# Weaving the two expert layers of neighbouring steps in a graph-and-experts kernel, with gate scores of two tiles in one bank and masks ten chunks ahead

## The chip, the cores and the metric

The kernel runs on one core of one Trainium2 chip. The time is device microseconds of one execution of the whole program, the median over several executions. Next to it stands one profiled execution, from which every row, wait and window below is read.

## What is computed

A graph layer is followed by a layer of eight experts, of which each node uses two. There are 6250 nodes with 256 features and 106,250 edges, sorted by their target node.

```python
deg = jnp.maximum(segment_sum(ones, dst, 6250), 1.0)
norm = deg ** -0.5
h = layernorm(x) @ W.T + b                      # 256 -> 256
x = x + norm * segment_sum((norm * h)[src], dst, 6250)
y = layernorm(x)
top, idx = top_k(y @ Wg.T + bg, 2)              # 8 experts, 2 for each node
p = softmax(top)
for e in range(8):                              # 256 -> 1024 -> 256
    x = x + combine(p, idx, e) * (relu(y @ W1[e].T + b1[e]) @ W2[e].T + b2[e])
```

## The kernel before

The prologue counts the degrees, scales the nodes and writes them to HBM as a table (`table`). Then the main loop runs over the edges in 831 chunks of 128, one chunk to a slot `s` of the program. The order of all work is written out by hand: what follows is put into the engines' queues in the order in which this loop calls it, and each engine takes its own queue in order.

**A slot.** It issues the gather of chunk `s + 6` on GpSimd (`gather`, L403: 128 rows of the table into one of 24 `rows` buffers), builds the mask of chunk `s + MASKS` on VectorE (`mask`, L410, MASKS is 6) and adds chunk `s` up on TensorE (`add_up`, L417: mask times rows into the bank `ps`). A row buffer comes free when its chunk has been added up, so gathers can lead TensorE by at most 24 chunks. A mask buffer comes free eight chunks after its use (`bufs=MASKS + 8`).

**Tasks of a tile.** A tile is 128 nodes, and 17 chunks on average hold the edges of one. From the slot at which its sums are complete, tasks follow at fixed distances (`STAGES`, L659): the sum is turned (L505), goes through the linear layer (`linear`, L517), gets its scores, chooses two experts (VectorE), is ranked (L585, L586), sorted by expert (`sort`, L649) and sent to queues in HBM, one for each expert (`send`, L672, eight stores on SyncE). The graph layer's part of the scores comes from `linear`; the part of the input `x` is worked out for two tiles at a time, early in the loop, by `inputs_turned` (L449, L452) and two slots later `inputs_scored` (L456 to L462). The latter takes one tile `ph` for each of the two node tiles, four matmuls into it, and one ScalarE copy of 128x8 out of it (L462).

**Steps.** A step is 256 queued rows of one expert (128 rows in the first nine and the last six steps of the 60). `choose` picks the expert, `load_first` (L723), `load_rows` (L732) and `load_second` (L737) load the first weights `w1` (1028 KB), the rows `xT` and the second weights `w2` (1152 KB). `up` (L757 to L767) is one of eight pieces of the first layer: four matmul instructions into one of the two `ph` banks, and a ReLU on ScalarE that empties it into `hid`. `down` (L769 to L780) is one of eight pieces (four for 128 rows) of the second layer, four matmul instructions into `py`; `leave` adds the bias on VectorE and stores to `yq`. `w1`, `w2` have three buffers each, `hid` two, `xT` four.

**The planner.** `next_piece` (L879) runs all `up` pieces of step `done` and then all its `down` pieces; `cur` counts them. The main loop (L894 to L912) gives each slot a credit of SLOT - CHUNK = 1025 (nanoseconds, less the planned cost `busy` of the slot's tasks), keeps at most SPARE = 2000 of it, and issues pieces while credit is positive and the step is `ready`: its `w2` has been issued and slot `earliest[step]` is reached. A piece is charged 915 (`up`) or 870 (`down`) for 256 rows. In steady state steps are due 17 slots apart.

**The tail.** After the last chunk (L913 on) one piece is issued in each turn, and between them the results are read back from `yq` by indirect gathers on GpSimd (`read_back`, L857), weighed and added (L865), and stored. `DONE` says after which step which tiles may be read. Loads are kept three steps ahead of `done` and `gone` (L934 to L943).

Of the kernel before, what the change touches and what calls it, by code (L numbers as in the profile page):

```python
# [7 lines left out]
F32 = mybir.dt.float32  # L8
# [6 lines left out]
AF = mybir.ActivationFunctionType  # L15
# [4 lines left out]
P = 128  # L20
# [8 lines left out]
NE = 8  # L29
H = 1024  # L30
HB = H // P
# [14 lines left out]
ROWS_OF = [n for s, n in STREAM] + list(TAIL)  # L46
USUAL = len(ROWS_OF)
# [7 lines left out]
PIECES = {FT: (915, 870), P: (600, 870)}  # L55
# [5 lines left out]
SPREAD = 4.0  # L61
AHEAD = 6
UP = 2.0 ** 11
MASKS = 6
ROWS = 24
HC = 64
GROUP = 7
# [6 lines left out]
LATER = 1 << 17  # L74
TURNED, PLACED, SORTED, SENT = 5, 17, 22, 24
LEAD = (13, 12)


COPIES = 3
# [70 lines left out]
def in_order(ctx: ExitStack, tc: tile.TileContext, g: Shared):  # L150

    nc = tc.nc
# [190 lines left out]
    psp = ctx.enter_context(tc.tile_pool(name="fpsp", bufs=2, space=PSUM))  # L343
# [6 lines left out]
    wg = keep.tile([P, 2, NE], F32, name="wg")  # L350
# [8 lines left out]
    xg = keep.tile([P, NT, NE], F32, name="xg")  # L359
# [7 lines left out]
    t0 = 0  # L367
    for step, t1 in DONE:
        nc.vector.memset(bounds[:, t0:t1, :], float(START[step + 1]))
        t0 = t1  # L370
# [83 lines left out]

    def inputs_scored(t0, t1):
        xT = turned_inputs.pop(t0)  # L456
        for t in range(t0, t1):
            px = psp.tile([P, NE], F32, name="ph")
            for k in range(2):
                nc.tensor.matmul(px, xT[:, k, (t - t0) * P:(t - t0 + 1) * P], wg[:, k, :],  # L460
                                 start=(k == 0), stop=(k == 1))
            nc.scalar.activation(xg[:, t, :], px, AF.Copy)  # L462

    kept = {w: (WINDOWS[w - 1][0] % P, WINDOWS[w][0] - WINDOWS[w - 1][0]) for w in range(1, len(WINDOWS))}
    keeps = {}
# [209 lines left out]
    steps = {}  # L675
# [63 lines left out]
    def fetch(step):  # L739

        for _ in choose(step):
            yield
            if step in steps and "w1" not in steps[step] and step < done + (cur >= HB) + 3:
                load_first(step)
        while "w1" not in steps[step]:
            if step < done + (cur >= HB) + 3:
                load_first(step)
            else:
                yield
        while sent < steps[step]["known"]:  # L750
            yield
        load_rows(step)
        while step >= gone + 3:
            yield
        load_second(step)

    def up(step, b):  # L757
        f = steps[step]
        w1 = f["w1"]
        n = ROWS_OF[step]  # L760
        if b == 0:
            f["hid"] = work.tile([P, HB, FT], F32, name="hid")
        ph = psp.tile([P, FT], F32, name="ph")
        for k in range(2):
            nc.tensor.matmul(ph[:, :n], w1[:, k * H + b * P:k * H + (b + 1) * P], f["xT"][:, :n, k],  # L765
                             start=(k == 0), stop=(k == 1))
        nc.scalar.activation(f["hid"][:, b, :n], ph[:, :n], AF.Relu, bias=w1[:, 2 * H + b:2 * H + b + 1])  # L767

    def down(step, i, s):  # L769
        f = steps[step]  # L770
        a = i // 4
        if i % 4 == 0:
            f["py"] = psp.tile([P, D], F32, name="py")
        for b in (2 * (i % 4), 2 * (i % 4) + 1):
            nc.tensor.matmul(f["py"], f["hid"][:, b, a * P:(a + 1) * P], f["w2"][:, b * D:(b + 1) * D],  # L775
                             start=(b == 0), stop=(b == HB - 1))
        if i % 4 == 3:
            plan_at(s + 1, leave, step, a, f["py"], f["w2"])
        if i == 4 * ROWS_OF[step] // P - 1:
            del steps[step]  # L780
# [32 lines left out]
    earliest, busy = {}, {}  # L813
# [17 lines left out]
    s = 1  # L831
# [12 lines left out]
    chosen = loaded1 = loaded2 = len(STREAM)  # L844
    all_sent = FROM[NT - 1] + SENT + 1

    cur = 0
    done = gone = 0

    def results(t0, t1, bound):  # L850

# [21 lines left out]
        if t1 == NT:  # L873
            engine.dma_start(g.out[(NT - 1) * P:N, :], g.xr[:LAST, NT - 1, :])

    def ready(s):
        return done < USUAL and "w2" in steps.get(done, {}) and s >= earliest.get(done, 0)

    def next_piece(s):  # L879

        nonlocal cur, done
        step = done
        if not ready(s):
            return
        if cur < HB:
            up(step, cur)
        else:
            down(step, cur - HB, s)
        cur += 1
        if cur == HB + 4 * ROWS_OF[step] // P:  # L890
            done += 1
            cur = 0

    with tc.manual_schedule():  # L894
        with rowp as rowpool:
            for c in range(AHEAD):
                gather(c)
            for c in range(MASKS):
                mask(c)
            credit = 0  # L900
            for s in range(NC):
                if s + AHEAD < NC:
                    gather(s + AHEAD)
                if s + MASKS < NC:
                    mask(s + MASKS)
                add_up(s)
                for fn, args in tasks.pop(s, []):
                    fn(*args)
                credit = min(credit + SLOT - CHUNK - busy.get(s, 0), SPARE)
                while credit > 0 and ready(s):  # L910
                    credit -= PIECES[ROWS_OF[done]][cur >= HB]
                    next_piece(s)  # L912
        with tc.tile_pool(name="ftail", bufs=2) as pool:  # L913
            s = NC
            pend = []
            plan = list(DONE)
            got = asked = allowed = stored = 0
            latest = 0
            since = {}

            def take():
                nonlocal got, stored
                t, j, yb = pend.pop(0)[1]
                add_in(t, j, yb)
                got += 1
                if got == 2 * stored + 11:
                    store(stored, stored + 4, nc.gpsimd)
                    stored += 4

            while done < USUAL or tasks or len(plan) > 1 or asked < 2 * allowed or pend:  # L930
                for fn, args in tasks.pop(s, []):
                    fn(*args)
                if s > all_sent and s > max(STREAM)[0] + 6:
                    if chosen < min(USUAL, done + 4):  # L934
                        run(choose(chosen))
                        chosen += 1
                    if loaded2 < min(loaded1, gone + 3):
                        load_second(loaded2)
                        loaded2 += 1
                    if loaded1 < min(chosen, done + (cur >= HB) + 3):  # L940
                        load_first(loaded1)
                        load_rows(loaded1)
                        loaded1 += 1  # L943
                was = done
                next_piece(s)
                if done > was:
                    since[was] = s
                if len(plan) > 1 and done > plan[0][0] and s >= since.get(plan[0][0], 0) + 6 \
                        and asked == 2 * allowed:
                    step, t1 = plan.pop(0)  # L950
                    results(allowed, t1, float(START[step + 1]))
                    allowed = t1
                    latest = step
                if asked < 2 * allowed and s % (4 if s > all_sent else 2):
                    pend.append((s, read_back(pool, rowat, asked // 2, asked % 2, latest)))
                    asked += 1

                if pend and (done == USUAL or len(pend) > 10 or s >= pend[0][0] + 8):
                    take()
                s += 1  # L960

            results(allowed, NT, float(START[USUAL]))
            late = work.tile([P, NT, 2], F32, name="late", bufs=1)
            missed = work.tile([P, 2], F32, name="missed")
            nc.vector.tensor_tensor(late, at, bounds, op=OP.is_ge)
            nc.vector.tensor_reduce(missed[:, 0:1], late, op=OP.add, axis=mybir.AxisListType.XY)
            nc.vector.tensor_reduce(missed[:, 1:2], most, op=OP.max, axis=mybir.AxisListType.X)
            nc.vector.tensor_scalar(missed[:, 1:2], missed[:, 1:2], float(SLOTS), None, op0=OP.is_gt)  # L970
            nc.vector.tensor_add(missed[:, 0:1], missed[:, 0:1], missed[:, 1:2])
            nc.vector.tensor_add(missed[:, 0:1], missed[:, 0:1], g.outside)
            ones = work.tile([P, 1], F32, name="ones")
# [547 lines left out]
```

## Time and profile before

| | |
|---|---|
| median of 3 runs | 1326.41 us (1326.34 to 1326.47) |
| the profiled execution | 1612.34 us, of which 1610.5 us is the span of the profile |
| mean granted TensorE clock in it | 0.879 |
| TensorE matmuls busy | 1241.0 us, 77% of the span |
| VectorE, ScalarE busy | 980.9 us (61%), 397.7 us (25%) |
| GpSimd busy | 901.2 us (56%) |
| gathers of the main loop | 831, 0.949 us each |

The profiled execution is 21.6% longer than the median run. Rows are read as: line, engine, operation, tiles written and read, shapes, count, busy time, mean length in ns, idle time of the engine just before, and what ended most of that idle time. A wait whose cause the profile doesn't show is put down to "issue" or "remote". `ph` is the tile of both `up` and `inputs_scored`.

### The profile page before, as it was taken

The page shows a single profiled execution, that of the slowest core. Times are in us where ns is not written, and L with a number is a line of the kernel's source. Part 1 is how long each engine was busy: PE and PEld are TensorE (multiplying, and loading weights), DVE is VectorE, ACT ScalarE, POOL GpSimd, SP SyncE. Part 2 cuts the span into 40 slices and gives each one's busy share as a digit, 9 for nine tenths or more (in the row PEclk, how much of TensorE's full clock was granted, in tenths as well). Part 3 has the DMA queues.
Part 4 walks back from the last instruction along what each step waited for, and adds up shares of the span by engine and source line. Part 5 has one row for each costly group of instructions (what it writes and reads, how often), then busy time and mean ns, then how long its engine had stood idle before and what let it go on. Part 6 is the DMA issues. An engine that isn't in the chain of part 4 may idle for free.

```text
span 1610.5 us, 24215 instructions
## 1 busy us (share of the span) xinstructions
PE 1241.0 (77%) x6304; PEld 937.4 (58%) x6304; DVE 980.9 (61%) x5416; ACT 397.7 (25%) x963; POOL 901.2 (56%) x983
## 2 busy tenths in 40 slices
PE   5237768874778898888888787889888888778894
PEld 5215546663556565655656565656656666567683
DVE  8711556665657676767667666666666665574542
ACT  1602222221221222222222222222222222121231
POOL 1075665656656566666666566656666664236533
PEclk9965767997979899999899898989899998988997
DMA  7432358785667666667767666757677676559784
GB/s 248 161 105 82 102 141 282 258 288 143 204 190 225 190 210 207 218 205 216 214 202 224 200 213 215 225 186 219 209 220 217 202 220 211 176 201 365 252 302 142
DMA packets 159197, 333.81 MB, mean 207 GB/s; under 512 B 26804, under 2 KB 105864, under 8 KB 143688
## 3 DMA queue, kind: packets, MB, share of 16 engines
q1 hardware_dynamic: 111372, 201.66, 37.0%
q0 software_dynamic: 46864, 129.82, 28.0%
q8 instruction: 52, 0.85, 0.2%
q14 instruction: 97, 0.79, 0.2%
q10 hardware_dynamic: 812, 0.68, 0.1%
HBM read 277.55 MB, written 54.50 MB: 206 GB/s over the span
## 4 chain that ended last, share of the span: by engine, by line
PE 56%; issue 11%; DVE 11%; another core or an unknown queue 11%; DMA 5%; ACT 3%; SPq 2%; POOL 1%; ACTq 0%; POOLq 0%; DVEq 0%
PE ph L765 23%; PE py L775 13%; PE ps L417 10%; PE pt L517 3%; PE ph L460 2%; DMA yb<-fyq,rowat 2%; DMA xT<-fhq 2%; ACT hid L767 1%; SPq L672 1%; PE px L649 1%; PE px L449 1%; PE pt L505 1%; PE count L216 1%; DVE mask L410 1%
## 5 line engine op out<-in xcount | busy, mean ns | idle before, releaser
L403 POOL DMA_INDIRECT rows<-ftable,src x831 | 789.0, 949 | 487.2 <-PE ps L417 190.0
L765 PE MATMUL ph<-xT,w 128*128 128x256 f32 (+1 forms) x1920 | 510.1, 405 | 189.4 <-issue 82.3
L765 PEld LDWEIGHTS ph<-xT,w 128*128 128x128 f32 x1920 | 366.4, 212 | 320.5 <-issue 146.4
L775 PE MATMUL py<-w,hid 128*128 128x256 f32 x1680 | 415.7, 381 | 0.0
L767 ACT ACTIVATE hid<-ph,w 128x256 f32<-128x256 f32 (+1 forms) x480 | 210.8, 446 | 633.8 <-PE ph L765 206.2
L775 PEld LDWEIGHTS py<-w,hid 128*128 128x128 f32 x1680 | 319.7, 191 | 70.3 <-issue 1.9
L417 PE MATMUL ps<-rows,mask 128*128 128x512 f16 x831 | 322.0, 416 | 42.8 <-DMA rows<-ftable,src 31.5
L410 DVE TENSOR_SCALAR mask<-col_b,rel 128x128 f16<-128x128 bf16 x831 | 200.8, 265 | 32.2 <-remote 11.7
L857 POOL DMA_INDIRECT yb<-fyq,rowat x98 | 94.6, 965 | 122.4 <-DMA w<-in_W 36.7
L417 PEld LDWEIGHTS <-mask 128*128 128x128 f16 x831 | 88.2, 109 | 76.9 <-issue 34.6
L524 DVE SCALAR_TENSOR_TENSOR xr<-pt,norm,xr 128x256 f32<-128x256 f32 x49 | 23.7, 483 | 151.4 <-PE pt L517 67.0
L787 DVE TENSOR_TENSOR y<-py,w 128x256 f32<-128x256 f32 x105 | 44.1, 420 | 101.5 <-PE py L775 35.4
L484 DVE SCALAR_TENSOR_TENSOR rolled<-rolled,keep,ps 128x256 f32<-128x256 f32 x149 | 70.7, 475 | 42.9 <-PE ps L417 23.3
L499 ACT ACTIVATE whole<-rolled 32x256 f32<-32x256 f32 (+2 forms) x156 | 63.9, 410 | 124.9 <-DVE rolled L487 61.6
L460 PE MATMUL ph<-wg,turned 128*128 128x8 f32 x196 | 40.8, 336 | 50.2 <-ACT turned L452 31.9
L460 PEld LDWEIGHTS ph<-wg,turned 128*128 128x128 f32 x196 | 39.6, 297 | 64.4 <-ACT turned L452 39.6
L487 DVE TENSOR_TENSOR rolled<-ps,rolled 128x256 f32<-128x256 f32 x150 | 63.7, 424 | 15.7 <-DVE rolled L484 6.8
L865 DVE SCALAR_TENSOR_TENSOR xr<-yb,prob,xr 128x256 f32<-128x256 f32 x98 | 45.7, 482 | 41.3 <-DMA yb<-fyq,rowat 40.1
L588 ACT ACTIVATE h2s<-h 128x256 f16<-128x256 f32 x49 | 20.3, 415 | 186.1 <-DVE h L579 104.5
L517 PE MATMUL pt<-gw,uT 128*128 128x264 f32 x196 | 61.9, 445 | 5.4 <-ACT uT L510 3.4
L517 PEld LDWEIGHTS pt<-gw,uT 128*128 128x128 f32 x196 | 44.4, 228 | 21.2 <-issue 5.5
L216 PE MATMUL count<-oh,ol 128*16 128x8 bf16 (+2 forms) x898 | 29.0, 174 | 21.8 <-DVE oh L205 18.0
(187 smaller groups left out, 1128.2 us busy)
## 6 DMA issues: line engine op xcount, KB each, us to landing
w<-in_W SPq DMA_DIRECT2D x60, 1152.0 KB
w<-in_W SPq DMA_DIRECT2D x60, 1028.0 KB
fhq<-ordered SPq DMA_DIRECT2D x392, 64.0 KB
fyq<-y SPq DMA_DIRECT2D x105, 128.0 KB
rows<-ftable,src POOLq DMA_INDIRECT x831
xT<-fhq SPq DMA_DIRECT2D x45, 256.0 KB
out<-xr POOLq DMA_DIRECT2D x11, 512.0 KB
xr<-in_x SPq DMA_DIRECT2D x6, 896.0 KB
```

The costliest lines, as they stand in the source:

```text
L403: nc.gpsimd.indirect_dma_start(out=rows[c], out_offset=None, in_=table[:, :], in_offset=bass.IndirectOffsetOnAxis(ap=g.src[:, c:c + 1], ax ...
L410: nc.vector.tensor_scalar(masks[c], g.col_b[:, r:r + P], g.rel[:, c:c + 1], None, op0=OP.is_equal)
L417: nc.tensor.matmul(sums[w], masks.pop(c), rows.pop(c), start=(c == chunks[0]), stop=(c == chunks[-1]))
L460: nc.tensor.matmul(px, xT[:, k, (t - t0) * P:(t - t0 + 1) * P], wg[:, k, :], start=(k == 0), stop=(k == 1))
L484: nc.vector.scalar_tensor_tensor(new, rolled, keeps[kept[w]], ps[:, 0:D], op0=OP.mult, op1=OP.add)
L487: nc.vector.tensor_add(new, ps[:, D:2 * D], new)
L499: nc.scalar.activation(whole[t][p0:p1, :], new[p0:p1, :], AF.Copy)
L517: nc.tensor.matmul(pl, uT[:, k, :], gw[:, k, :], start=(k == 0), stop=(k == 1))
L765: nc.tensor.matmul(ph[:, :n], w1[:, k * H + b * P:k * H + (b + 1) * P], f["xT"][:, :n, k], start=(k == 0), stop=(k == 1))
L767: nc.scalar.activation(f["hid"][:, b, :n], ph[:, :n], AF.Relu, bias=w1[:, 2 * H + b:2 * H + b + 1])
L775: nc.tensor.matmul(f["py"], f["hid"][:, b, a * P:(a + 1) * P], f["w2"][:, b * D:(b + 1) * D], start=(b == 0), stop=(b == HB - 1))
L857: r = nc.gpsimd.indirect_dma_start(out=yb, out_offset=None, in_=yq[0:START[upto + 1], :], in_offset=bass.IndirectOffsetOnAxis(ap=where[:, ...
```

## The change

A step's first layer is issued in turn with the second layer of the step before it. `next_kind` decides: if both an `up` piece of step `upped` and a `down` piece of step `done` may run, they alternate, with `up` first; an `up` may start only when the step before last is through its second layer (`upped <= done + 1`) and its rows have been issued. A `down` that hasn't begun waits when the next step's `up` is due within HOLD = 10 slots. `inputs_scored` puts the scores of two tiles into one `ph` tile and empties it with one ScalarE copy. MASKS goes from 6 to 10, and the mask buffers from 14 to 18. The conditions for loads are counted in `upped` in place of `done + (cur >= HB)`.

```diff
-MASKS = 6
+MASKS = 10
+HOLD = 10
...
     def inputs_scored(t0, t1):
         xT = turned_inputs.pop(t0)
+        px = psp.tile([P, 2, NE], F32, name="ph")
         for t in range(t0, t1):
-            px = psp.tile([P, NE], F32, name="ph")
             for k in range(2):
-                nc.tensor.matmul(px, xT[:, k, (t - t0) * P:(t - t0 + 1) * P], wg[:, k, :],
+                nc.tensor.matmul(px[:, t - t0], xT[:, k, (t - t0) * P:(t - t0 + 1) * P], wg[:, k, :],
                                  start=(k == 0), stop=(k == 1))
-            nc.scalar.activation(xg[:, t, :], px, AF.Copy)
+        nc.scalar.activation(xg[:, t0:t1, :], px[:, :t1 - t0], AF.Copy)
...
-            if step in steps and "w1" not in steps[step] and step < done + (cur >= HB) + 3:
+            if step in steps and "w1" not in steps[step] and step < upped + 3:
                 load_first(step)
...
-    def ready(s):
-        return done < USUAL and "w2" in steps.get(done, {}) and s >= earliest.get(done, 0)
+    def next_kind(s):
+
+        first = upped < USUAL and upped <= done + 1 and "xT" in steps.get(upped, {}) and s >= earliest.get(upped, 0)
+        second = done < upped and "w2" in steps.get(done, {})
+        if first and second:
+            return "down" if was == "up" else "up"
+        if first:
+            return "up"
+        soon = 0 < earliest.get(upped, 0) - s <= HOLD and upped <= done + 1 and curd == 0
+        return "down" if second and not soon else None

     def next_piece(s):

-        nonlocal cur, done
-        step = done
-        if not ready(s):
-            return
-        if cur < HB:
-            up(step, cur)
-        else:
-            down(step, cur - HB, s)
-        cur += 1
-        if cur == HB + 4 * ROWS_OF[step] // P:
-            done += 1
-            cur = 0
+        nonlocal curu, curd, done, upped, was
+        was = next_kind(s)
+        if was == "up":
+            up(upped, curu)
+            curu += 1
+            if curu == HB:
+                upped, curu = upped + 1, 0
+        if was == "down":
+            down(done, curd, s)
+            curd += 1
+            if curd == 4 * ROWS_OF[done] // P:
+                done, curd = done + 1, 0
+        return was
...
-                while credit > 0 and ready(s):
-                    credit -= PIECES[ROWS_OF[done]][cur >= HB]
-                    next_piece(s)
+                while credit > 0:
+                    of = upped, done
+                    kind = next_piece(s)
+                    if not kind:
+                        break
+                    credit -= PIECES[ROWS_OF[of[kind == "down"]]][kind == "down"]
...
-                    if chosen < min(USUAL, done + 4):
+                    if chosen < min(USUAL, upped + 4):
...
-                    if loaded1 < min(chosen, done + (cur >= HB) + 3):
+                    if loaded1 < min(chosen, upped + 3):
```

More of the change, by code (lines that the diff above doesn't have):

```diff
@@ L742, in fetch @@
             yield
-            if step in steps and "w1" not in steps[step] and step < done + (cur >= HB) + 3:
+            if step in steps and "w1" not in steps[step] and step < upped + 3:
                 load_first(step)
         while "w1" not in steps[step]:
-            if step < done + (cur >= HB) + 3:
+            if step < upped + 3:
                 load_first(step)
@@ L845, in in_order @@
     all_sent = FROM[NT - 1] + SENT + 1
-    cur = 0
-    done = gone = 0
+    curu = curd = 0
+    done = gone = upped = 0
+    was = None
     def results(t0, t1, bound):
@@ L874, in store @@
             engine.dma_start(g.out[(NT - 1) * P:N, :], g.xr[:LAST, NT - 1, :])
-    def ready(s):
-        return done < USUAL and "w2" in steps.get(done, {}) and s >= earliest.get(done, 0)
-    def next_piece(s):
-        nonlocal cur, done
-        step = done
-        if not ready(s):
-            return
-        if cur < HB:
-            up(step, cur)
-        else:
-            down(step, cur - HB, s)
-        cur += 1
-        if cur == HB + 4 * ROWS_OF[step] // P:
-            done += 1
-            cur = 0
+    def next_kind(s):
[7 more added lines that the diff above has]
+        return "down" if second and not soon else None
+    def next_piece(s):
+        nonlocal curu, curd, done, upped, was
[11 more added lines that the diff above has]
+        return was
     with tc.manual_schedule():
@@ L943, in in_order @@
                         loaded1 += 1
-                was = done
+                over = done
                 next_piece(s)
-                if done > was:
-                    since[was] = s
+                if done > over:
+                    since[over] = s
                 if len(plan) > 1 and done > plan[0][0] and s >= since.get(plan[0][0], 0) + 6 \
```

## The prediction

> **What bounds the kernel now.** I read the page first, then busy time by windows, then who waited for whom on TensorE and GpSimd, then the timeline of single slots and the chain of waits.
>
> The windows show a main loop in which one engine is nearly full:
>
> ```profile
> 1000.00:1100.00 100.00, 86.82 (x363) 64.03 (x364) 65.85 (x367) 25.62 (x62) 59.78 (x64) 0.90 0.67 204
> 1100.00:1200.00 100.00, 84.68 (x363) 62.51 (x362) 64.74 (x391) 24.21 (x58) 62.16 (x66) 0.91 0.69 213
> 1200.00:1300.00 100.00, 85.94 (x377) 63.41 (x376) 63.44 (x377) 22.64 (x54) 63.15 (x67) 0.93 0.70 219
> ```
>
> Columns are TensorE matmuls, weight loads, VectorE, ScalarE, GpSimd (busy us, instructions), granted clock, DMA share, GB/s. TensorE is busy 85 to 87%, and the fifth column counts the gathers: 64 to 67 in 100 us, 1.53 us a chunk, 26 us for the 17 chunks of a step.
>
> GpSimd isn't the bound of this execution; it waits for row buffers that TensorE hasn't emptied:
>
> ```profile
> L403 POOL DMA_INDIRECT rows<-ftable,src x831: 940/946/1191, 81.6 to 1357.9; - x167
>   PE ps L417: 190.0, 165
>   issue: 170.7, 536
>   remote: 64.6, 42
> ```
>
> But its own pace, when nothing holds it, is close behind:
>
> ```profile
> 98.21 0.95 POOL L403 DMA_INDIRECT rows<-ftable,src  x1 [0.30 <-issue]
> 99.46 0.95 POOL L403 DMA_INDIRECT rows<-ftable,src  x1 [0.30 <-issue]
> ```
>
> 1.25 us from start to start. The chain of waits gives TensorE's cost of undisturbed pieces:
>
> ```profile
> 819.98 0.90 PE ph L765 x4
> ...
> 822.89 0.22 PE ps L417
> 823.11 0.89 PE pt L517 x4
> ...
> 824.22 0.86 PE py L775 x4
> ```
>
> A first-layer piece takes 0.90 us, a second-layer piece 0.86, a chunk 0.22, `linear` 0.89. So 17 chunks with a step cost 17 x 0.22 + 8 x 0.90 + 8 x 0.86 = 17.8, plus `linear` 0.89, sort 0.45 and turning 0.22 from the same chain, and half of an input pair (1.57 planned for scoring and 0.43 for turning, so 1.0): 20.4 us, 1.20 us a chunk. TensorE undisturbed would be just quicker than the gathers (21.25 us for 17). It takes 26, because it stops:
>
> ```profile
> PE ph L765 <- issue: 74.8, 53, 5.9
> PE ph L765 <- ACT hid L767: 59.4, 25, 6.1
> PE ph L765 <- DMA xT<-fhq: 13.2, 9, 4.5
> PE ps L417 <- DVE rolled L487: 7.8, 2, 6.2
> ```
>
> These are TensorE's waits from 200 to 1350 us (us, times, longest). In that window it is idle 215 us (1150 less 934.5 busy, summed from the windows), and 134 us of it lie before first-layer pieces that wait for a ReLU, or for something unseen. Second-layer pieces wait for nothing. The timeline shows it: from 824.05 on, eight `down` pieces with their chunks run without a gap, while the `up` pieces of the same step, from 805.87, have holes of 3.8 and 0.7 us.
>
> **What the Trainium skill says.** "TensorE: Matmul & The Clock Gate", Part 1 on the HAM clock gate: after an idle window of about 3.4 us the array falls to half clock, and a busy window brings it back. The trace agrees: after the 3.8 us hole at 807.8 the matmuls start 0.43 us apart instead of 0.225, until about 819. So a hole is paid for again. The same page, on engine queue depths: ScalarE and VectorE are strict first-in first-out. Here too: the sort's eviction, the copies `whole`, `uT` and `h2s` (0.4 to 0.6 us each) stand in ScalarE's queue between the ReLUs, and `h2s` alone sat 94 us waiting for VectorE's `h`. "PSUM — Partial Sum Buffer", the four PSUM rules: a group's first matmul clears the written bits of its whole bank. Two score groups in one bank are safe as they run one after the other; no time follows from it.
>
> **Profiled time and median.** The sum below stands against the execution of 1612.34 us (span 1610.5 and 1.8 around it). The median is 286 us less, so most of these waits can't exist there, and a saving in the profile mustn't be carried over whole. I work out what is left. The first gather starts at 81.6. At 1.25 us, 831 gathers take 1039, so the loop ends at 1120, the last chunk 4 later. In the tail stand seven `down` pieces (6.0), seven steps of 256 rows at 14.1 (98.6), six of 128 rows at
>
> ```profile
> 1540.19 4.66 PE L765 MATMUL ph<-xT,w 128*128 128x128 f32 x32
> 1544.69 3.61 PE L775 MATMUL py<-w,hid 128*128 128x256 f32 x16
> ```
>
> about 8.3 (49.6), some 5 for the last tiles, and 22 from the last `down` piece (1589) to the end: 181. Together 1305, 1307 with the 1.8. Only 19 us of the median's 1326 are then losses that TensorE's order can reach. If the 0.30 us between gathers, or part of it, is due to profiling, TensorE itself is the limit: 656 chunks with full steps save 0.05 each (33), and the 175 before them about 17, the floor is 1257 and 69 us can be reached. I take the middle, 44.
>
> **The change part by part.**
>
> *Weaving.* It adds and removes no instruction. Between two `up` pieces now lies a `down` piece (0.86) and often a chunk (0.22), so a ReLU (0.47) may come up to 1.08 us later before its bank is missed. The 78 waits of the two first rows average 1.7 us; at most 78 x 1.08 = 84 us go, 39% of the 215 idle. Clock lost after a hole goes along, so I take 45% of what is reachable: 9 us of 19, 31 of 69, 20 in the middle. What is late next: the rows `xT` (13 us now), and then GpSimd, whose 1.25 us end all further gain.
>
> *What moves with it.* `down` of a step comes about 17 slots later, and with it two VectorE adds (0.42 each) and two `yq` stores on SyncE. `w2` of step k is asked for at the same slot as before; it needs the buffer of step k-3, whose last `down` now ends some 9 slots before. SyncE would wait only if it ran 9 slots ahead of TensorE; behind it stand the stores of sorted rows and `xT`. I take 0, with 0 to +10 as bounds. `hid` needs the `down` of step k-2, some 4 slots earlier in TensorE's own order: 0. `py` gets twice the time for its eviction, which nobody waited for.
>
> *The end of the loop.* Following the planner's credits slot by slot: the old order has issued 709 pieces at slot 831 (step 46, nine of sixteen), the new one 701 (five of `up` 46, four of `down` 45), because the first steps' `down` pieces are held for a partner. Eight pieces, 8 x 0.86 = 7 us, move into the tail, which gets eight turns longer. If TensorE never catches up with the gathers this costs nothing, since it would have had to do them anyway; if it does, it costs 7. Against it, 48 `up` pieces of 128 rows take 4.66/8 = 0.58 us, while four instructions at 0.11 are 0.45: ScalarE paces them. Half of them now have a `down` beside them: 24 x 0.13 = 3 us back. Sum 0 to +4; +4 at the slow end.
>
> *Scores of two tiles in one bank.* 49 copies of 0.177 us become 25: 4.3 us of ScalarE, an engine 25% busy, before 250 us. TensorE waited for this copy once, 3.9 us. Bounds -4 and +1 (the first tile's bank stays taken longer); I take -1.
>
> *Masks ten ahead.* Same 831 instructions of 0.25 us; TensorE waited for a mask for under 2 us. Four more stand before the loop's first VectorE work, 1 us. Where VectorE is held by `add_sums` (51, 44 and 32 us of waits for TensorE in the main loop) chunks have four more masks in hand. Bounds -5 and +1, taken -1.
>
> Sum: -20 (weaving), +4, -1, -1: -18; I take -16, since part of the regained time runs into the gathers' pace: 1310. In the profiled execution, where TensorE is behind to the end, I expect more, some 70 to 100 us off the span.
>
> **Rivals.** *The gathers pace the unprofiled loop.* Then weaving recovers nothing there: for it speaks that 1307 lies so near the median, against it that GpSimd waits 190 us for TensorE. The eight pieces in the tail cost 7, less the 3 of small steps: 1330, slower. It decides from the point where TensorE is level with the gathers at the last chunk (less than some 7 us behind; it is 31 behind in the profile). *Holes and half clock dominate in the median too.* Then weaving takes two thirds of 69, and more by clock: about 1270. For it: 134 of 215 idle us sit at `up`; against it, the 286 us that vanish without the profiler. *The change does little*: the holes are ones that the trace puts down to "issue", lasting 3 to 6 us, longer than one `down` piece covers: gains and the tail cancel, 1326.
>
> **How the numbers follow.** Forecast (1280 to 1322, taken as 1310) 0.58; holes dominate (below 1280) 0.12; nothing within 0.2%, which is about what a measurement of this kernel can tell from no change, 0.10; gathers pace and the tail pays 0.20. Faster 0.70, same 0.10, slower 0.20. The range goes from 1272, into the second rival, to 1333, the slower one with its full 7 us.
>
> **What would show it.** In the profile after: waits of `ph` L765 for ReLUs and "issue" under 70 us in place of 134; no hole over 3.4 us inside a step, mean clock above 0.9; gathers at over 70 in 100 us; GpSimd's wait for `ps` well under 190; the tail, from the last gather on, no more than 7 us longer. Wrong it would be if the waits move to `xT` or to SyncE's `w2` load, or if the profile gets much shorter and the median doesn't.

## The result and the profile after

| | before | after |
|---|---|---|
| median, same chip | 1326.44 us (1326.34 to 1328.00) | 1340.24 us (1338.33 to 1342.39) |
| ratio, 95% interval | | 1.0102 (1.0084 to 1.0119) |
| a profiled execution | 1328.3 us span, clock 0.959 | 1340.5 us span, clock 0.959 |

The change costs about 14 us; slower was the case with a chance of 0.20. The span of 1328.3 us is of a second profile of the kernel before, `e0_before_again`: the execution of 1612.34 us that the prediction was read from is of another kind than the median's (further down a set, which is a group of kernels measured together with the kernel before, met that kind again, with the kernel before at 1587.8 us), so only the second profile can be set beside the one after.

First the page of after: busy time, share of the span and instructions of each engine (PE is TensorE), and the granted clock in tenths over 40 slices.

```profile
PE 1154.7 (86%) x6304; PEld 896.9 (67%) x6304; DVE 986.4 (74%) x5416; ACT 397.6 (30%) x939; POOL 903.2 (67%) x983
...
PEclk9999867998989999999999999999999998989996
```

Read against the first profile of before (1610.5 us, 77%, 0.879) everything the change was to bring seems to be there: a span 270 us shorter, a fuller TensorE, a higher clock. The second profile of before shows them too, without the change (1328.3 us, 87%, 0.959). Busy time by windows, after and then the kernel before, columns as in the prediction:

```profile
1000.00:1100.00 100.00, 94.25 (x445) 71.17 (x444) 75.78 (x450) 27.44 (x67) 75.72 (x80) 1.00 0.82 256
1100.00:1200.00 100.00, 86.16 (x380) 68.98 (x381) 71.39 (x412) 24.24 (x56) 56.12 (x59) 0.93 0.79 271
1200.00:1300.00 100.00, 97.73 (x511) 85.24 (x510) 51.01 (x223) 29.19 (x70) 54.12 (x57) 1.00 0.87 308
```

```profile
1000.00:1100.00 100.00, 95.10 (x451) 72.62 (x449) 76.22 (x454) 28.29 (x66) 75.93 (x80) 1.00 0.83 258
1100.00:1200.00 100.00, 86.81 (x391) 69.14 (x389) 71.07 (x407) 25.32 (x59) 61.56 (x65) 0.95 0.82 275
1200.00:1300.00 100.00, 99.62 (x523) 85.47 (x522) 54.29 (x245) 31.97 (x78) 53.65 (x57) 1.00 0.90 333
```

In the main loop both make 80 gathers in 100 us, 1.25 us each, where the first profile of before had 64. The gather's own rows (durations min/median/max, first and last start, and below them idle time of GpSimd before a gather and how often), after and before, say that the loop ends at the same time in both:

```profile
L404 POOL DMA_INDIRECT rows<-ftable,src x831: 942/946/1183, 81.7 to 1126.1; - x167
  issue: 115.5, 378
  PE ps L418: 56.7, 186
```

```profile
L403 POOL DMA_INDIRECT rows<-ftable,src x831: 942/946/1187, 81.8 to 1127.2; - x167
  issue: 109.0, 357
  PE ps L417: 64.5, 209
```

The idle times put down to `ps` are 0.31 us each on average: nearly all of it is the 0.30 us that stand before every gather, and not waits for TensorE like those of the first profile (190.0 us in 165).

And TensorE's longest waits from 160 to 1120 us, after and then before, are for the gathered rows and for `xT`:

```profile
PE ps L418 <- DMA rows<-ftable,src: 39.0, 48, 2.7
PE ph L766 <- DMA xT<-fhq: 26.6, 24, 2.3
```

```profile
PE ps L417 <- DMA rows<-ftable,src: 34.2, 37, 3.1
PE ph L765 <- DMA xT<-fhq: 27.0, 25, 4.2
```

No wait of `ph` for a ReLU stands in either list, where the first profile had 59.4 us and 74.8 us more put down to "issue". So the loop had nothing that the weave could regain: GpSimd paces it. The loss comes after the last gather, which ends at 1127.1 us after and 1128.2 before.

### The profile page after: what moved, and what is told of

Its sections match the earlier page's. It is cut to its first block, busy times and chain, and to the rows that moved or that the text cites. A ratio compares the mean times of both kernels' runs of the same rounds, so it can differ in the third digit from the quotient of the medians.

```text
span 1340.5 us, 24208 instructions
## 1 busy us (share of the span) xinstructions
PE 1154.7 (86%) x6304; PEld 896.9 (67%) x6304; DVE 986.4 (74%) x5416; ACT 397.6 (30%) x939; POOL 903.2 (67%) x983
## 5 line engine op out<-in xcount | busy, mean ns | idle before, releaser
L766 PE MATMUL ph<-xT,w 128*128 128x256 f32 (+1 forms) x1920 | 468.4, 368 | 36.4 <-DMA xT<-fhq 36.1
L776 PE MATMUL py<-w,hid 128*128 128x256 f32 x1680 | 436.9, 383 | 2.3 <-DVE y L788 1.7
L766 PEld LDWEIGHTS ph<-xT,w 128*128 128x128 f32 x1920 | 342.8, 193 | 138.8 <-issue 54.4
L768 ACT ACTIVATE hid<-ph,w 128x256 f32<-128x256 f32 (+1 forms) x480 | 214.3, 447 | 712.9 <-PE ph L766 625.1
L418 PE MATMUL ps<-rows,mask 128*128 128x512 f16 x831 | 309.9, 400 | 79.4 <-DMA rows<-ftable,src 74.6
L776 PEld LDWEIGHTS py<-w,hid 128*128 128x128 f32 x1680 | 317.5, 191 | 86.5 <-issue 20.9
L411 DVE TENSOR_SCALAR mask<-col_b,rel 128x128 f16<-128x128 bf16 x831 | 208.3, 272 | 8.3 <-PE ps L418 8.2
L418 PEld LDWEIGHTS <-mask 128*128 128x128 f16 x831 | 84.6, 105 | 77.4 <-issue 39.9
L867 DVE SCALAR_TENSOR_TENSOR xr<-yb,prob,xr 128x256 f32<-128x256 f32 x98 | 46.0, 482 | 63.2 <-DMA yb<-fyq,rowat 62.5
L518 PE MATMUL pt<-gw,uT 128*128 128x264 f32 x196 | 54.8, 405 | 0.0
L518 PEld LDWEIGHTS pt<-gw,uT 128*128 128x128 f32 x196 | 39.3, 201 | 16.9 <-issue 6.8
L217 PEld LDWEIGHTS <-ol 128*16 128x16 bf16 x898 | 28.7, 109 | 22.2 <-DVE ol L203 16.1
```

Of the source, the lines that this page charges most:

```text
L217: nc.tensor.matmul(counts[k][:, u - k * GROUP * 8:v - k * GROUP * 8], ol[:, :, i], oh[:, u - first:v - first, i], start=False, stop=(c0 + ...
L411: nc.vector.tensor_scalar(masks[c], g.col_b[:, r:r + P], g.rel[:, c:c + 1], None, op0=OP.is_equal)
L418: nc.tensor.matmul(sums[w], masks.pop(c), rows.pop(c), start=(c == chunks[0]), stop=(c == chunks[-1]))
L518: nc.tensor.matmul(pl, uT[:, k, :], gw[:, k, :], start=(k == 0), stop=(k == 1))
```

## The tail, piece by piece

The hole at step 49 comes first. The loads of that step can't be asked for until the last tile has been sent, so TensorE runs out of work there in both kernels. Its timeline (start, length, in brackets the idle time before and its releaser), after:

```profile
1175.01 1.07 PE L766 MATMUL ph<-xT,w 128*128 128x256 f32 x4
1175.91 1.02 PE L776 MATMUL py<-w,hid 128*128 128x256 f32 x4
1184.82 2.05 PE L766 MATMUL ph<-xT,w 128*128 128x256 f32 x4 [7.89 <-DMA xT<-fhq]
1186.67 1.91 PE L776 MATMUL py<-w,hid 128*128 128x256 f32 x4
```

and before:

```profile
1169.78 7.07 PE L775 MATMUL py<-w,hid 128*128 128x256 f32 x32
1183.85 9.29 PE L765 MATMUL ph<-xT,w 128*128 128x256 f32 x32 [7.01 <-DMA xT<-fhq]
```

Before, the eight `down` pieces of step 48 are done (the first line, 32 instructions) when TensorE stops. After, the piece at 1175.01 is the last of the first layer of step 48, the one at 1175.91 the last of the second layer of step 47, and all eight `down` pieces of step 48 stand behind the waiting `up` of step 49, the first of them at 1186.67: 7 us of work that had no one to wait for. The Trainium skill ("TensorE: Matmul & The Clock Gate", Part 1) states that the array falls to half clock after about 3.4 us without work. The trace agrees: behind the 7.9 us of this hole a piece takes twice its time for some microseconds (2.05 for 1.07).

From there I split the rest of each span in two: from the first `up` of step 49 to the last `down` of step 59, and from that to the end. The third figure is how much later than the end of its last matmul each bias addition `y` of steps 49 to 59 ended, summed over the 16 of them (undisturbed it is 0.5 us each, 8 in all). The numbers are worked out from the trace of each kernel, one profile each.

| kernel | step 49 starts | to the last `down` | to the end | span | `y` late, summed |
|---|---|---|---|---|---|
| before (`e0_before_again`) | 1183.9 | 120.4 | 24.0 | 1328.3 | 44 |
| `e3_no_weave` | 1181.0 | 121.2 | 22.8 | 1325.0 | 45 |
| after | 1184.8 | 129.6 | 26.1 | 1340.5 | 62 |
| after (`f0_after_again`) | 1184.4 | 127.2 | 25.8 | 1337.4 | 64 |
| `e2_tail_serial` | 1180.2 | 127.6 | 21.3 | 1329.2 | 96 |
| `e1_hold0` | 1180.8 | 132.6 | 21.7 | 1335.1 | 42 |
| `f1_down48_first` | 1190.3 | 118.8 | 26.0 | 1335.1 | 66 |
| `f2_add_later` | 1180.2 | 125.8 | 21.3 | 1327.3 | 31 |
| `f3_serial_add_later` | 1180.3 | 126.3 | 20.3 | 1326.9 | 85 |
| `g0_both` | 1190.3 | 116.1 | 20.9 | 1327.3 | 18 |
| `h0_hold0_add_14` | 1179.8 | 128.8 | 21.1 | 1329.7 | 29 |
| `g2_after_add_4` | 1185.3 | 149.1 | 27.8 | 1362.2 | 136 |
| `g3_before_add_4` | 1180.3 | 136.4 | 29.4 | 1346.1 | 149 |
| `g1_before_add_later` | 1177.0 | 120.0 | 23.8 | 1320.8 | 45 |
| `h1_before_add_22` | 1178.8 | 120.3 | 19.9 | 1319.0 | 8 |

The labels are those of the experiments below; `e3_no_weave` runs its pieces in the order of the kernel before, and `f0_after_again` is the changed kernel once more. Two profiles of the same order differ by up to 3 us in these columns, and by up to 5 in when the loop's last chunk ends (1132.3 us in `g1_before_add_later`, 1137.0 in the first row), so single rows aren't read more closely than that.

Of the 12.2 us between before and after 0.9 is in the start, 9.2 in the stretch (6.8 by `f0_after_again`) and 2.1 in the end. Eight pieces less what the small steps give back are 7 - 3 = 4; so 3 to 5 of the stretch and the 2 of the end are something else. TensorE waits in the stretch for 3.9 us after (1.7 for `y`, 2.2 for rows and weights) and for 0.3 before. The chain of waits (start, length, what) leads to a cause, after first and then before:

```profile
1276.01 0.42 DVE y L788
...
1277.46 9.04 DMA fyq<-y
1286.57 0.70 issue
1287.27 0.94 POOL yb L859
1288.21 0.21 issue
1288.52 5.17 DMA yb<-fyq,rowat
1293.74 0.41 issue
1294.15 0.26 DVE xr L867
...
1295.47 0.42 DVE y L788
...
1297.07 7.10 DMA fyq<-y
```

```profile
1256.62 0.47 PE ph L765 x4
...
1269.06 3.45 PE py L775 x16
...
1277.01 3.45 PE py L775 x16
...
1284.95 3.45 PE py L775 x16
```

Before, TensorE itself is the chain until about 1290. After, the chain as the trace follows it, from 1253 us on, holds no piece of either layer. It goes in a ring: a bias addition on VectorE, its store, a read-back of that row, the addition of the read-back (`xr`) on VectorE, and only behind it the next bias addition. VectorE takes its queue in order, so an `xr` that waits for its read-back, for up to 9.8 us, holds every `y` behind it, and a late `y` makes the next read-back late. Not all of the chain is this ring: 11.9 us of it, up to 1267, are idle time of GpSimd put down to "issue", and `f0_after_again` has some pieces of both layers in its chain. So the ring is a suspect that the experiments have to try. VectorE's waits from 1178 us on, after and before:

```profile
DVE xr L867 <- DMA yb<-fyq,rowat: 62.3, 35, 9.8
```

```profile
DVE xr L865 <- DMA yb<-fyq,rowat: 49.8, 35, 6.6
```

## The experiments

Ratios are to the kernel before in the same set, with 95% intervals.

**Is there anything to gain in the loop?** The kernel before with a profile once more, and the kernel before with only the masks and the scores of the change (its edits of `MASKS` and `inputs_scored`, nothing else).

> The kernel before, unchanged, profiled once more. The profile of the kernel after spans 1340.5 us, 2 us under its median time, while the first profile of before is 284 us over its median. If the first profile was a disturbed execution and the loop really is paced by the gathers, the new span is about 1324 us, GpSimd issues 80 gathers in every 100 us (1.25 us each, 1039 in all) and waits for TensorE's chunks for under 20 us. If TensorE does bound it, gathers come at under 75 in 100 us here too.

> Before with the two small edits alone: masks ten ahead, gate scores of two tiles in one bank. Theories D and T: 1325 to 1328 us, no change. If the edits themselves cost (a later start of the first chunks, a bank held longer early on): 1330 to 1340.

`e0_before_again`: 1330.06 us, its profile is the one above. `e3_no_weave`: 1328.96 us, ratio 1.0000 (0.999 to 1.0009). The gathers come at 80 in 100 us, as the reading of a paced loop asked; the idle time put down to `ps` isn't under 20 us, but above it is seen to be something else. Masks and scores do nothing that can be measured, so the loss is the weave's, with the conditions for choices and loads that go with it.

**Which part of the weave costs?** `e1_hold0` lets the loop issue as many pieces as the kernel before (709 before slot 831) and keeps the tail woven; `e2_tail_serial` keeps the loop of the change and finishes each step's `down` pieces first in the tail.

```diff
-HOLD = 10
+HOLD = 0
```

```diff
     def next_kind(s):
...
+        if s >= NC and second:
+            return "down"
         if first and second:
```

> After with HOLD = 0: in the main loop each step's second layer is no longer held for a partner, so there the order is that of before, 709 pieces are issued before slot 831 as before (701 after), and only the tail stays woven; masks and gate scores as after. Theory D (the eight deferred pieces and their shift of the tail are the loss): 1324 to 1329 us, as before. Theory T (weaving in the tail itself, later results, reads and stores that collide at the end, is the loss): 1336 to 1341. Theory M (woven order slows the main loop or the masks or scores do): the last chunk's time tells; M by the masks or scores would stay at 1340.

> After, but from slot 831 on a second-layer piece that may run always goes first, so steps run one after the other in the tail; the main loop stays woven and still ends eight pieces behind. Theory D: the eight pieces remain, so 1333 us or more (7 us over before), with 1340 if they are all of it. Theory T: back to about 1326 to 1331. If both have a part: between, and e1 and e2 together give the parts.

`e1_hold0`: 1338.15 us, 1.0084 (1.0061 to 1.0107). That is Theory T's range, and Theory D falls as the only cause. Taking the put-off pieces back changes little, since they are not needed to make the tail bad: TensorE's hole there is

```profile
PE ph L766 <- DMA xT<-fhq: 13.3, 1, 13.3
PE py L776 <- DVE y L788: 5.3, 1, 5.3
```

with the `down` pieces of step 48 behind it all the same. `e2_tail_serial`: 1332.08 us, 1.0037 (1.0020 to 1.0053). More than half of the loss goes with the woven order of the tail alone, though eight pieces are still put off. The time lies between the two theories, so both have a part. The last column of the table is no measure of it: `e2_tail_serial` has its `y` 96 us late in sum and is faster than `e1_hold0` with 42. Lateness costs only where TensorE or the end waits for it.

**Is it the pieces behind the hole, or the additions?** `e4`/`f1` let step 48 end before step 49 begins; `e5`/`f2` put the additions of read-backs (L867) 14 turns after their gather in place of 8 (a turn is one pass of the tail's loop, which issues one piece); `e6`/`g0` do both; `e7`/`f3` join the later additions with the serial tail.

```diff
+        if second and upped == 49 and curu == 0:
+            return "down"
```

```diff
-                if pend and (done == USUAL or len(pend) > 10 or s >= pend[0][0] + 8):
+                if pend and (done == USUAL or len(pend) > 10 or s >= pend[0][0] + 14):
```

> After, with one exception to the alternation: the second layer of step 48 goes ahead of the first layer of step 49, whose loads can't be asked for before slot 862. Theory Q (in-order queue: eight ready pieces, 7 us, stand behind one piece that waits 7.9 us for its rows) says the wait falls from 7.9 to about 1 us and the time to 1332 to 1335. The rival (a fixed amount of weights and read-backs through the DMA engines bounds the tail, whatever TensorE's order) says 1338 to 1341, with the idle time only moved to later steps.

> After, with each read-back's weighed add put into VectorE's queue 14 turns after its gather in place of 8 (or when eleven are pending, as before). Theory V (adds that wait for their read-backs hold VectorE, so the bias adds behind them free py late and store late, and TensorE and the next read-backs wait): waits of py for y go from 1.7 us to 0 and stores land earlier; 1334 to 1338. The rival (DMA bound) says no change or later stores, 1339 to 1343.

> After with both edits (step 48's second layer ahead of step 49, adds 14 turns later). If Q and V are separate costs they add: 1327 to 1331, level with before. If the DMA engines bound the tail: no better than the better of the two alone.

> The kernel with the woven main loop and the serial tail (1332 us) with the adds 14 turns later. There TensorE waits 6.1 us for y before py, and nothing else. Theory V: that wait goes, 1325 to 1328, level with before or just under. Rival: the wait is for DMA capacity and stays, 1331 to 1334.

In the set of `e4` to `e7` the kernel before took 1587.8 us (1573 to 1602), an execution of the first profile's kind, and all four were faster than it: `e4` 1577.23, 0.9954 (0.9927 to 0.9981); `e5` 1573.89, 0.9896 (0.9842 to 0.9949); `e6` 1567.28, 0.9879 (0.9819 to 0.9938); `e7` 1562.84, 0.9859 (0.9813 to 0.9905). The set can't explain the loss, which it doesn't contain, but it tests the prediction's own reading. TensorE's longest waits from 160 to 1350 us in `e4`:

```profile
PE ph L766 <- DMA xT<-fhq: 35.5, 17, 5.1
PE ph L766 <- issue: 31.5, 25, 3.2
PE ph L766 <- ACT hid L768: 23.1, 9, 5.0
```

Those before a ReLU or put down to "issue" are 54.6 us in place of the first profile's 134, so the weave does seem to cover ReLUs where there are any to cover (the kernel before has no profile in this set, and `e4` has an edit of its own). But waits for `xT` grew from 13.2 to 35.5 us, and the time fell by 11 us in `e4` and 25 in `e7`, not by the 70 to 100 that the prediction expected of such an execution. The four went again as `f1`, `f2`, `f3` and `g0`, with the changed kernel beside them as `f0`.

> After, unchanged, as the reference of this set. The same kernel before took 1326 us in two sets and 1588 us in the third, so times are compared within a set alone. If before takes about 1327 here, after takes 1338 to 1342. If before takes about 1590 here (an execution like that of the first profile, in which ReLUs start microseconds after their piece), the forecast's own reasoning should hold: TensorE is behind the gathers, weaving covers late ReLUs, and after is faster than before by 10 to 30 us.

> After with step 48's second layer ahead of step 49's first. In a set where before takes 1327: Theory Q (in-order queue) 1332 to 1335, rows' wait 1 us in place of 7.9; the rival (DMA engines bound the tail) 1338 to 1341. In a set where before takes 1590 the 7 us are within the spread.

> After with each read-back's add 14 turns after its gather in place of 8. In a set where before takes 1327: Theory V (waiting adds hold VectorE, and the bias adds and stores behind them) 1334 to 1338; rival (DMA bound) 1339 to 1343.

> Woven main loop, serial tail, adds 14 turns later. In a set where before takes 1327: Theory V 1325 to 1328, the wait of py for y (6.1 us in the serial tail) gone; rival 1331 to 1334. In a set where before takes 1590: about 1563 again, 1.4% under before.

> After with both edits (step 48's second layer ahead of step 49's first; adds 14 turns after their gathers). The adds alone brought after to before's time (1327.7), the other edit alone only 2 us. If the hole at step 49 (5.1 us left) is a cost of its own once VectorE is free: 1321 to 1325, faster than before. If the tail is then bound by its transfers: 1326 to 1329.

| | median us | ratio (95%) |
|---|---|---|
| `f0_after_again` | 1339.30 | 1.0083 (1.0053 to 1.0113) |
| `f1_down48_first` | 1336.93 | 1.0059 (1.0041 to 1.0076) |
| `f2_add_later` | 1327.72 | 1.0005 (0.9989 to 1.0022) |
| `f3_serial_add_later` | 1329.49 | 1.0010 (0.9997 to 1.0024) |
| `g0_both` | 1328.36 | 1.0004 (0.9992 to 1.0017) |

Filling the hole brings some 2 us by the medians, less than Theory Q asked for, and the intervals of `f0` and `f1` overlap. In `f1` the longest wait for `xT` falls to 1.0 us, and another wait comes up:

```profile
PE py L776 <- DVE y L788: 6.0, 1, 6.0
```

The idle time moved. That `y`, at 1183.75, isn't held by a read-back: from 1168 on VectorE works through the choices of four steps (`choose`, L682 on, some 3.5 us each), which stand ahead of it in the queue.

Six turns more for the additions bring 12 us by the medians, 10 by the ratios. That is more than Theory V asked for, and with the same transfers, so the rival that transfers bound the tail whatever the order falls. No order of pieces adds to it; `g0` has the same wait for `y` of 6 us as `f1`, so it doesn't show whether transfers bound what is left. In the table above `f2`'s stretch is 125.8, within 1.4 us of the 120.4 + 4 that the pieces alone ask for (TensorE waits 1.3 in it), and its `y` are half as late.

**Is that a repair of the change, or a gain that any version gets?** The kernel before with 14 turns, and both kernels with 4 (the same edit of the same line, 8 to 14 and 8 to 4).

> The kernel before with the adds 14 turns later, nothing woven. If waiting adds cost before as well: 1318 to 1323, and then weaving itself still costs some 5 us in after. If before's adds fit at 8 turns, and only the woven tail made them late: 1325 to 1328, no change.

> After with the adds only 4 turns after their gathers. Theory V (VectorE in order behind waiting adds) says slower still, 1345 to 1365, with more VectorE wait for read-backs than after's 61 us. If what helped at 14 was something else (other order of gathers and stores), 1338 to 1341.

> The kernel before with adds 4 turns after their gathers, the control of the last. If before has room in VectorE that the woven tail lacks: 1326 to 1332. If it has none either: 1335 or more, the same slope as after.

| turns from gather to addition | before | after |
|---|---|---|
| 4 | 1348.39, 1.0162 (1.0133 to 1.0191) | 1358.18, 1.0224 (1.0199 to 1.0248) |
| 8 | 1327 | 1339.30, 1.0083 (1.0053 to 1.0113) |
| 14 | 1323.88, 0.9970 (0.9962 to 0.9978) | 1327.72, 1.0005 (0.9989 to 1.0022) |

Both. The additions are a cost of the kernel before as well, and cutting the turns to 4 makes it slower than the change ever did. VectorE's waits from 1178 us on in `g3_before_add_4`:

```profile
DVE xr L865 <- DMA yb<-fyq,rowat: 86.8, 48, 9.5
```

But the curve is steeper where the change sits: from 8 to 14 turns before gains 3 us and after 12. The difference between the kernels is 10, 12 and 4 us at 4, 8 and 14 turns by the medians, 8, 11 and 5 by the ratios, each uncertain by 2 to 5 us. So some 6 to 8 us of the loss come by way of the additions, and 4 to 5 stay. The lateness of `y` agrees: from 8 to 14 turns it falls from 62 to 31 us after, and stays before (44 and 45). By what way the kernel before gains its 3 us isn't shown: its stretch and its end are the same at 8 and 14 turns, and of the 7 us by which step 49 starts earlier in that profile, 5 are there already at the last chunk, which the edit doesn't reach.

**What are the 4 to 5 that stay?** `h0_hold0_add_14` takes the put-off pieces back (HOLD = 0) in a kernel with 14 turns. `h1_before_add_22` asks how far the additions can be moved, with room for them.

```diff
-        yb = pool.tile([P, D], F32, name="yb", bufs=12)
+        yb = pool.tile([P, D], F32, name="yb", bufs=18)
...
-                if pend and (done == USUAL or len(pend) > 10 or s >= pend[0][0] + 8):
+                if pend and (done == USUAL or len(pend) > 16 or s >= pend[0][0] + 22):
```

> The order before slot 831 is that of the kernel before (no pieces of down put off past it), the tail stays woven, and the read-back adds come 14 turns after their gather. Theory A, the last few us of the loss are the eight pieces of down that were put off into the tail (7 us of TensorE): 1322 to 1325, ratio 0.996 to 0.999, near the kernel before with adds at 14 (1323.9). Theory B, they come from the woven order in the tail itself: 1327 to 1330, ratio 1.000 to 1.002, as with the deferred pieces.

> The kernel before with the read-back adds 22 turns after their gather instead of 8, with room for them in the queue of adds and in the read-back buffers. Theory A, VectorE's waits for read-backs still cost something at 14 turns: 1320 to 1323, ratio 0.995 to 0.997. Theory B, at 14 turns what the adds held up is gone and the end is set by TensorE and by the sums that come later for the last rows: 1323 to 1327, ratio 0.997 to 1.000.

`h0_hold0_add_14`: 1330.27 us, 1.0033 (1.0020 to 1.0045). Theory A falls: without put-off pieces it is not faster than `f2`, its ratio is 0.3% higher. Its timeline has the reason:

```profile
1167.59 1.02 PE L776 MATMUL py<-w,hid 128*128 128x256 f32 x4
1179.82 2.04 PE L766 MATMUL ph<-xT,w 128*128 128x256 f32 x4 [11.20 <-DMA xT<-fhq]
1181.66 1.91 PE L776 MATMUL py<-w,hid 128*128 128x256 f32 x4
```

Having no put-off work it comes to step 49 earlier, waits 11.2 us for rows that can't come sooner, and has seven of step 48's eight `down` pieces (6 us) behind the wait, each again a partner of an `up`. With `HOLD` = 10 the pieces are late because they were put off, with 0 because they are woven; either way some eight pieces lie behind the hole that the kernel before has ahead of it. Theory B is the nearer one for this kernel, whose time lies just above its range. But where the pieces stand isn't shown to be the cause: `g0` has them ahead of step 49 and is no faster than `f2`, as TensorE waits 6.1 us for `y` there. For the serial tail Theory B says nothing: `f3` has no hole and nothing behind it, and still loses 5 to 6 us against `g1`; its `y` are 85 us late in sum and TensorE waits 5.5 us for them. The traces suggest why VectorE is later there, though no run tests it: in `f3` four choices of steps stand ahead of the first `y` of step 48 (at 1183.46), in the kernel before three (1178.70), and that kernel then stands in its hole, in which VectorE catches up. The fourth is let in by the change itself: it chooses while `chosen < upped + 4`, the kernel before while `chosen < done + 4`, and `upped` is one ahead of `done` while a second layer runs. So the cause of these 4 to 5 us stays open.

`h1_before_add_22`: 1320.16 us, 0.9956 (0.9940 to 0.9973), the fastest of all, 6 us under the kernel before. Theory A holds: VectorE's longest waits from 1178 us on have changed sides.

```profile
DVE y L787 <- PE py L775: 43.8, 15, 7.6
DVE xr L865 <- DMA yb<-fyq,rowat: 12.9, 10, 2.5
```

It now waits for TensorE, no `y` ends more than 0.6 us after its last matmul, and the end after the last `down` is 19.9 us in place of 24.0. The change with 22 turns was not tried.

## Why the prediction was wrong

- **Profiled time and median: the step that failed first.** It saw that the waits of a profile of 1612 us "can't exist" in a median of 1326, worked out that 19 us could be reached if the gathers pace the loop and 69 if not, and took the middle, 44. The second profile, whose execution is as long as the runs without one, has the 0.30 us between gathers too, so there was no other side to take a middle with. And hardly any of the 19 was lost to late ReLUs: the last gather ends at 1128.2, not 1120 (1.26 us each), which is 8 of them; 7.0 is the hole at step 49, and 2 the half clock behind it (9.29 us for the `up` pieces that take 7.25 in the next step).
- **Weaving, -20: nothing.** 45% was taken of what was not there. In the kind of execution that it was read from, the wait was judged about right and the time wasn't: waits for ReLUs and "issue" under 70 us were asked for, and `e4` had 54.6, but 70 to 100 us were to come off, and the woven kernels there gained 11 to 25, with other edits in them.
- **Masks and scores, -1 each.** Together 0, within 1.3 us (`e3`). Right that they are near nothing. Of the three waits named for `add_sums`, the 32 us are put down to "issue" in the trace, not to TensorE.
- **The end of the loop, 0 to +4.** Eight pieces move into the tail, as the planner's credits said. The first rival was to decide where TensorE is less than some 7 us behind the gathers at the last chunk; it is 8.8 us behind in the second profile, 6.1 in that of `e3` and 9.9 in that of after, so at the border, where the first profile had 31. A difference of the size of +4 is left between `f2` and `g1` (1327.72 against 1323.88), but by `h0` putting the pieces off isn't its cause: without putting off it was not less. That the size agrees is in part luck.
- **What moves with it, 0: the term that failed in size.** Without it the first rival's 1330 is still 10 us short. Named were two VectorE additions and two stores of a step that come later, with nobody waiting for them. It left out what stands in VectorE's queue around those additions, the read-back additions, which wait for the very rows that the moved additions write. The step says that `py` has an eviction "which nobody waited for"; the ring `y`, store, read-back, `xr` goes through it. By the runs with 8 and 14 turns it measured some +6 to +8.
- **Rivals.** That the gathers pace the loop was right in its mechanism and in its sign, and given 1330 against 1340. That little would happen was wrong, and that holes dominate too.
- **What would show it.** Gathers at 80 in 100 us, clock 0.959, a wait of GpSimd for `ps` of 57 us in place of 190: all as asked for, and all in the kernel before as well (80, 0.959 and 64.5). A hole of over 3.4 us stands at step 49 (7.9), and from the last gather to the end the tail is 13 us longer, not 7. The line that counted was the last one: the profile gets much shorter and the median doesn't.

## What to carry to other kernels

Before anything is read from a profile, its length is held against the unprofiled runs; where they differ by a fifth, its waits are another execution's, and the first thing to buy is a second profile. An instruction that waits for the end of a long path must not stand in an in-order queue ahead of those that feed the path: put it some turns later, as far as buffers allow, and measure the distance, since with 4, 8, 14 and 22 turns the kernel before took 1348, 1327, 1324 and 1320 us. When two chains of work are woven, look for the waits that the engine will have anyway and see what the weave leaves standing behind them.

## What the runs showed that I had not expected

The same program takes 1324 to 1333 us in most executions and 1573 to 1612 us in others, with gathers of the same length, 946 ns in both. It went by the set: all 23 runs of the kernel before beside `e4` to `e7` were of the long kind, and all 95 beside the other experiments of the short one. Each of these sets ran on another chip; whether the chip is the reason isn't shown. What differs, where I looked, is how late an engine starts on another's signal. Worked out from the ReLUs of the first layer, from the end of their piece to their start, the 90th percentile is 0.09 us in `e0_before_again`, 3.79 in the first profile and 4.38 in `e4`; the longest is 0.39 us in the first of these and 10.06 in the second. In the long kind the woven kernels that ran are faster than the kernel before by 0.5 to 1.4%, each with another edit besides. Whether the change as it stands is faster there too was not tried, and what makes the signals late is not seen in the traces.
